# Scan steps moved 1500 places ahead in the scheduler's order, and a back-stage slab that is refilled with the next image pair

## The chip, the cores and the metric

The kernel runs on one core of one Trainium2 chip. The metric is the device time of one execution in microseconds (us). Times of a kernel are given as the median of several runs. A profile is one execution recorded by the hardware profiler; it has a span of its own.

The engines that appear below: PE (TensorE, matrix products; its weight loads are PEld), DVE (VectorE), ACT (ScalarE), POOL (GpSimd), and SP (SyncE), which here only issues DMA transfers.

## What is computed

Four layers are applied to `x` of shape 8 x 64 x 64 x 64 (images, channels, rows, columns), all in float32:

- layer 0: a pixel-attention block with 1x1 and depthwise 3x3 convolutions and batch norms,
- layer 1: two window-attention blocks (8 x 8 windows, 8 heads, the second shifted by 4), each with an MLP,
- layer 2: a dynamic 3x3 filter, then a 1 x 9 convolution,
- layer 3: a selective scan over the 4096 pixels in four directions, a gated norm and projection, then a multi-scale modulation (max pools, depthwise convolutions, GELU).

The scan is the long part. Cut to what matters:

```python
def _selective_scan(xs, dts, A, Bs, Cs, D):
    ...
    def step(h, inp):
        u_t, dt_t, B_t, C_t = inp
        h = h * jnp.exp(dt_t[..., None] * A) + dt_t[..., None] * B_t[:, :, None, :] * u_t[..., None]
        return (h, jnp.einsum('bkcn,bkn->bkc', h, C_t))
    h0 = jnp.zeros(u.shape[1:] + (A.shape[-1],), u.dtype)
    _, ys = jax.lax.scan(step, h0, (u, dt, Bl, Cl))
    return jnp.moveaxis(ys, 0, -1) + D[None, :, :, None] * xs
...
y = out_y[:, 0] + inv[:, 0] + wh + invwh
```

There are 128 channels, 16 states a channel, and 4 directions for each image.

## The kernel before

**Stages.** The eight images are worked in four pairs. A pair passes through `front(p)` (layer0, layer1, layer2, then `scan_sources`, which makes the inputs of the scan: `xc`, its transposed `xt`, and the gate `zs`, all written to DRAM for each image), then `scans(p)` (the selective scan of both images), then `back(p)` (norm, gate, projection and the multi-scale modulation). The main program runs `front(0)` alone and then, for p = 0 to 3, `scans(p)` with other work beside it: `back(p-1)` and then `front(p+1)`, chained in one generator, `beside`. In `scans(3)` there is no front left; `back(2)` lies beside it and `back(3)` is fed in over its last units (`late`) and finished behind it.

**A scan step.** `scans(p)` has 64 units (image, direction k, chunk c of 512 pixels), each of 8 steps, so 512 steps. A step handles two of the 16 states. It consists of two loads by SP that spread one pair of rows over the partitions (B and C, `fetch`, L1801), a product on POOL (`products`, L1809, into `vd`, eight buffers), and in `step`: two exponentials on ACT (L1831), two DVE scan instructions (L1834), two copies of the last column into `carries` on ACT (L1838), and two products with C (L1842), one on POOL and one on DVE; in every fourth step both are on DVE when `own` is 2, which holds for the last two images and while `self.dense` is set. `sums` (L1854) adds the products up on PE in a PSUM bank `yd`. For a unit there are also `load` (the chunk `xs`), `inputs` (two products on PE, exponential and logarithm on ACT, `rows` to DRAM), `spread` (`du`, four transfers) and `gather` (adds `yd` into `Y` on DVE, and in the fourth direction writes `ys`).

**Order.** The code is written in a program order, step by step; the framework's scheduler then places instructions engine by engine. Each instruction has a priority, which is its place in the program. Of the instructions whose inputs and buffers are ready, the scheduler takes the one with the earliest priority. Each engine then executes its queue in the order that was built. `with tc.high_priority(offset=n)` gives the instructions within it a priority n places earlier; it changes no dependence and no amount of work.

In program order `scans` puts, in each step i, the fetches of steps i+3 and i+2, the step, the sums due, and then draws from `beside` as much as its share of the cost: the front and back work spread over all but the last `LEAD` = 24 steps.

**Memory.** `slabs` has three large buffers (128 x 4356 float32). The front and the back stage take them in turn: X, `att`, `VT`, `XP`, `taps`, `H`, `XI`, `XT` in the front; X3, F and `big` in the back stage. A new slab waits until an old one has been released. `layer0` begins with a single 2 MB load of X into a new slab (L1293). `back` loads X3, `y` and `z` by chunks of 512 columns; `y` and `z` lie in the first four eighths of `big`, the same four for each chunk. PSUM banks for the work beside the scans come from the pool `pf` alone; while `front(0)` runs alone (`self.alone`, `turn`), both pools are used and the accumulators of `total` alternate between two banks.

The loop that sets the program order:

Of the kernel before, what the change touches and what calls it, by code (L numbers as in the profile page):

```python
# [18 lines left out]
CH = 512  # L19
# [6 lines left out]
NTD = L // TD  # L26
GRP = 2
LEAD = 24
TC = 1024
NTC = L // TC  # L30
SLAB = 66 * 66
# [1128 lines left out]
class _Direct:  # L1160
# [8 lines left out]
    def __init__(self, net, ctx):  # L1169
        self.net, self.tc, self.nc, self.w = net, net.tc, net.nc, net.w  # L1170
        tc = self.tc
        self.dram = ctx.enter_context(tc.tile_pool(name="mem", bufs=2, space=bass.MemoryType.DRAM))
        self.slabs = ctx.enter_context(tc.tile_pool(name="slabs", bufs=3))
        self.ps = ctx.enter_context(tc.tile_pool(name="ps_scan", bufs=3, space=PSUM))
        self.pf = ctx.enter_context(tc.tile_pool(name="ps_front", bufs=3, space=PSUM))
        self.kept = {}
        self.turn = -1
        self.alone = self.others = False
        self.dense = 0
        self.rows_done = 0  # L1180

    def begin(self, ctx):

# [98 lines left out]
    def front(self, p):  # L1282
# [2 lines left out]
        yield from self.layer2(X)  # L1285
        yield from self.scan_sources(p, X)

    def layer0(self, p):


        nc, tc, w, net, half = self.nc, self.tc, self.w, self.net, self.HALF
        X = self.flat("X")
        nc.sync.dma_start(X, self.net.x[2 * p : 2 * p + 2].rearrange("b c h w -> (b c) (h w)"))  # L1293
        att = self.padded("att")
        VT = self.flat("VT").rearrange("p (t c) -> p t c", c=P)

        def at(rows, t):
            return X[rows, t * P : (t + 1) * P]

        with self.work("w0") as wk:  # L1300
            for g in range(8):
                pv = self.bank("pval", (P, 4, P))
                nc.tensor.matmul(pv, lhsT=net.ones[0:1, :], rhs=net.b1row.rearrange("o a c -> o (a c)").unsqueeze(1).to_broadcast([1, 4, P]), start=True, stop=False)
                for j in range(4):
                    nc.tensor.matmul(pv[:, j, :], lhsT=at(slice(0, P), 4 * g + j), rhs=net.w1bd, start=False, stop=(j == 3))
                nc.scalar.activation(VT[:, 4 * g : 4 * g + 4, :], pv, AF.Relu)
                yield 3

            parts = wk.tile([P, 2, 32, NCH], F32, name="parts", tag="parts", bufs=1)
            self.dense = 1  # L1310
            for jc in range(NCH):
                po = self.total("po")
# [26 lines left out]
                nc.vector.tensor_copy(self.rows(att, jc), self.img(po))  # L1339

            self.dense = 0
            sums = net.sums[:, p]
            nc.vector.tensor_reduce(sums, parts, AX.X, ALU.add)
            rec = wk.tile([P, 2, 32], F32, name="rec", tag="rec", bufs=1)
            nc.vector.reciprocal(rec, sums)
            for g in range(8):
                pr = self.bank("prec")
                for j in range(4):
                    for im in range(2):
                        nc.tensor.matmul(  # L1350
                            pr[half[im], j * P : (j + 1) * P],
                            lhsT=rec[:, im, 4 * g + j : 4 * g + j + 1].to_broadcast([P, 64]),
                            rhs=w["ident"],
                            start=True,
                            stop=True,
                        )
                d = self.rows(att, g)
                nc.vector.tensor_tensor(d, d, self.img(pr), ALU.mult)
                yield 3
        with self.work("w0b") as wk:  # L1360
            diag = self.spread_taps(wk, w["dw2"])
            for c in range(NCH):
                acc = self.bank("cacc", (P, 8, 64))
                yield from self.taps_sum(acc, diag, att, 8 * c, 1.56, wt=w["dw2"], n=5)
                cv = wk.tile([P, 8, 64], F32, name="cv", tag="cv")
                nc.scalar.activation(cv, acc, AF.Relu, scale=net.bn23[:, 0:1], bias=net.bn23[:, 1:2])
                pw = self.bank("pw")
                nc.tensor.matmul(pw, lhsT=w["w3bd"], rhs=cv, start=True, stop=True)
                nc.scalar.activation(pw, pw, AF.Identity, scale=net.bn23[:, 2:3], bias=net.bn23[:, 3:4])
                x = X[:, c * CH : (c + 1) * CH]  # L1370
                nc.vector.tensor_tensor(x, x, pw, ALU.add)
                yield 2.25
        return X
# [339 lines left out]
    def scans(self, p, beside, cost):  # L1713
# [16 lines left out]
        steps = [{} for _ in range(n)]  # L1730
        done = 0
        for i in range(-3, n):
            if i + 3 < n:
                self.fetch(i + 3, steps[i + 3], 0)
            if 0 <= i + 2 < n:
                self.fetch(i + 2, steps[i + 2], 1)
                self.products(i + 2, steps[i + 2])
            if i >= 0:
                self.step(i, steps[i])
                for j in self.DUE[i % 8]:  # L1740
                    if i + j >= 0:
                        self.sums(i + j, steps[i + j], steps[i]["w"])
                if i % 8 == 2 and i > 8:
                    self.gather(self.units[i // 8 - 1])
                if p == B // 2 - 1 and done >= cost:
                    self.turn = max(self.turn, 0)
                while done < cost * (i + 1) / (n - LEAD):
                    done += next(beside, cost)
            if late and i >= n - 8 * (NTD - 1) and i % 8 in (3, 5, 7):
                next(late)  # L1750
            if i >= 0 and i % 8 < 3 and i // 8 + 1 < len(self.units):
                (self.load, self.inputs, self.spread)[i % 8](self.units[i // 8 + 1])
        for i in (n - 2, n - 1):
            self.sums(i, steps[i])
        self.gather(self.units[-1])
# [120 lines left out]
    def back(self, p):  # L1876
        nc, tc, w, net, half = self.nc, self.tc, self.w, self.net, self.HALF
        out = net.out[2 * p : 2 * p + 2].rearrange("b c h w -> (b c) (h w)")
        X = self.flat("X3")
        F = self.padded("F")  # L1880
        big = self.flat("big")
        with tc.tile_pool(name="w4", bufs=2) as wk:
            for c in reversed(range(NCH)):
# [1 line left out]
                nc.sync.dma_start(X[:, cols], self.kept["x", p][:, cols])  # L1885
                po = self.bank("po3")
                for im in range(2):
                    y = self.share(big, im)
                    z = self.share(big, 2 + im)
                    nc.sync.dma_start(y, self.kept["y", 2 * p + im][:, cols])  # L1890
                    nc.sync.dma_start(z, self.kept[2 * p + im][2][:, cols])
                    pc, sd = self.normed(wk, lambda pc: [(pc, y)], w["cen128"], w["avg128"], net.eps[:, 0:1])
                    u = wk.tile([P, CH], F32, name="u", tag="u")
                    nc.vector.scalar_tensor_tensor(pc, pc, w["on_g"], sd, ALU.mult, ALU.mult)
                    nc.vector.scalar_tensor_tensor(u, pc, w["on_b"], z, ALU.add, ALU.mult)
                    nc.tensor.matmul(po[half[im]], lhsT=w["opT"], rhs=u, start=True, stop=True)
                    yield 4.2
# [6 lines left out]
        with tc.tile_pool(name="w5", bufs=1) as wk:  # L1904
# [48 lines left out]
            for c in range(NCH):  # L1953
# [34 lines left out]
                nc.vector.tensor_tensor(pa, pa, self.rows(F, c), ALU.mult)  # L1988
                nc.vector.tensor_tensor(X[:, cols], X[:, cols], pa.rearrange("p a b -> p (a b)"), ALU.add)
                nc.sync.dma_start(out[:, cols], X[:, cols])  # L1990
                yield 3.5
            net.log_exp(last)


# [49 lines left out]
```

## Time and profile before

| | us |
|---|---|
| median of 3 runs | 11730.94 (11729.53 to 11735.17) |
| the profiled execution, reported time | 11724.67 |
| its span in the profile | 11722.8 |
| opening with `front(0)`, until the first scan | 1560 |
| `scans(0)` with `front(1)` | 1560 to 4103 |
| `scans(1)` with `back(0)`, `front(2)` | 4103 to 6872 |
| `scans(2)` with `back(1)`, `front(3)` | 6872 to 9644 |
| `scans(3)` with `back(2)` and `back(3)` | 9644 to 11723 |

Over the span PE is busy 83%, DVE 72%, ACT 60% and POOL 59%. The profile's costliest groups are those of the scan steps; each line shows source line, engine, operation, output from inputs, shapes, count, then busy time and mean duration, then the idle time of the engine just before them and what ended most of it:

```profile
L1809 POOL TENSOR_TENSOR vd<-B,du 128x1024 f32<-128x1024 f32 x2048 | 4801.7, 2363 | 2896.0 <-DMA B<-rows 1732.7
L1842 POOL TENSOR_TENSOR vd<-hd,C 128x512 f32<-128x512 f32 x1737 | 2210.8, 1278 | 1765.4 <-DVE hd L1834 1719.2
L1834 DVE TENSOR_TENSOR_SCAN dad<-dad,carry,vd 128x512 f32<-128x512 f32 x2064 | 2602.0, 1275 | 228.4 <-ACT dad L1831 224.8
L1842 DVE TENSOR_TENSOR vd<-dad,C 128x512 f32<-128x512 f32 x2359 | 1559.6, 673 | 167.9 <-ACT carry L1838 128.7
```

A step thus holds 2.36 us of product on POOL, with 1.28 us more when POOL does one of the two multiplies, and on DVE two scans of 1.27 us and at least one multiply of 0.67 us. A float32 matrix product stands twice in the profile (two passes), so counts of PE rows are twice the program's instructions. "Window rows" below are the 16 calls of `window_row` in a front, eight for each block of layer1.

### The profile page before, as it was taken

The page shows a single profiled execution, that of the slowest core. Times are in us where ns is not written, and L with a number is a line of the kernel's source. Part 1 is how long each engine was busy: PE and PEld are TensorE (multiplying, and loading weights), DVE is VectorE, ACT ScalarE, POOL GpSimd, SP SyncE. Part 2 cuts the span into 40 slices and gives each one's busy share as a digit, 9 for nine tenths or more (in the row PEclk, how much of TensorE's full clock was granted, in tenths as well). Part 3 has the DMA queues.
Part 4 walks back from the last instruction along what each step waited for, and adds up shares of the span by engine and source line. Part 5 has one row for each costly group of instructions (what it writes and reads, how often), then busy time and mean ns, then how long its engine had stood idle before and what let it go on. Part 6 is the DMA issues. An engine that isn't in the chain of part 4 may idle for free. (4 is left out here: it accounts for less than half of the span.)

```text
span 11722.8 us, 161838 instructions
## 1 busy us (share of the span) xinstructions
PE 9682.2 (83%) x55454; PEld 3278.2 (28%) x55454; DVE 8416.8 (72%) x9856; ACT 7078.9 (60%) x16513; POOL 6924.2 (59%) x3799
## 2 busy tenths in 40 slices
PE   9987899998879779998888969999888976655556
PEld 2244332223332222222442213222333221111111
DVE  0033368887777685778777775878778669989998
ACT  5545367766664756776665665776666465555554
POOL 0000058876665565777555574777556558778994
PEclk9998989999999889999999879999998977877677
DMA  0000055553444554555333463555334356556663
GB/s 21 1 2 2 27 164 176 172 174 118 128 124 123 168 165 128 167 169 164 103 113 110 140 201 102 171 166 173 120 106 129 109 172 196 171 177 200 205 205 120
DMA packets 779781, 1577.06 MB, mean 135 GB/s; under 512 B 89280, under 2 KB 89408, under 8 KB 778176
## 3 DMA queue, kind: packets, MB, share of 16 engines
q1 hardware_dynamic: 736320, 1443.18, 40.6%
q10 hardware_dynamic: 42624, 123.44, 3.7%
q8 instruction: 438, 7.18, 0.2%
q14 instruction: 399, 3.27, 0.1%
HBM read 1197.16 MB, written 100.66 MB: 111 GB/s over the span
## 5 line engine op out<-in xcount | busy, mean ns | idle before, releaser
L1809 POOL TENSOR_TENSOR vd<-B,du 128x1024 f32<-128x1024 f32 x2048 | 4801.7, 2363 | 2896.0 <-DMA B<-rows 1732.7
L1842 POOL TENSOR_TENSOR vd<-hd,C 128x512 f32<-128x512 f32 x1737 | 2210.8, 1278 | 1765.4 <-DVE hd L1834 1719.2
L1854 PE MATMUL yd<-vd,pack 128*64 128x512 f32 x8192 | 2684.9, 691 | 602.0 <-POOL vd L1842 501.5
L1831 ACT ACTIVATE dad<-du,As 128x512 f32<-128x512 f32 x4096 | 2719.1, 682 | 635.5 <-DVE vd L1842 412.5
L1834 DVE TENSOR_TENSOR_SCAN dad<-dad,carry,vd 128x512 f32<-128x512 f32 x2064 | 2602.0, 1275 | 228.4 <-ACT dad L1831 224.8
L1834 DVE TENSOR_TENSOR_SCAN hd<-dad,carry,vd 128x512 f32<-128x512 f32 x1520 | 1922.7, 1266 | 347.5 <-ACT dad L1831 298.2
L1842 DVE TENSOR_TENSOR vd<-dad,C 128x512 f32<-128x512 f32 x2359 | 1559.6, 673 | 167.9 <-ACT carry L1838 128.7
L1324 PE MATMUL s<-X 64*128 64x512 f32 x4096 | 1542.2, 644 | 74.9 <-ACT e L1330 68.9
L1330 ACT ACTIVATE e<-s 128x512 f32<-128x512 f32 x2048 | 1197.3, 589 | 468.1 <-PE s L1324 467.8
L1854 PEld LDWEIGHTS yd<-vd,pack 128*64 128x64 f32 x8192 | 651.9, 151 | 2292.6 <-issue 1169.1
L1316 PE MATMUL po<-e,VT 128*64 128x512 f32 x4096 | 1264.5, 620 | 9.5 <-ACT e L1330 8.7
L1838 ACT ACTIVATE carry<-dad 128x1 f32<-128x1 f32 x2063 | 345.8, 169 | 903.4 <-DVE dad L1834 804.4
L1324 PEld LDWEIGHTS s<-X 64*128 64x128 f32 x4096 | 422.2, 186 | 1181.4 <-issue 831.3
L1838 ACT ACTIVATE carry<-hd 128x1 f32<-128x1 f32 x1521 | 303.1, 200 | 678.4 <-DVE hd L1834 669.8
L1483 PE MATMUL w_av<-wide,vals 64*32 64x64 f32 x16384 | 502.6, 227 | 127.3 <-DVE w_oc L1512 74.2
L1483 PEld LDWEIGHTS w_av<-wide,vals 64*32 64x32 f32 x16384 | 416.7, 113 | 258.9 <-issue 138.6
L1316 PEld LDWEIGHTS po<-e,VT 128*64 128x64 f32 x4096 | 250.5, 135 | 841.0 <-issue 565.7
L1471 ACT ACTIVATE wide<-wide 128x512 f32<-128x512 f32 x512 | 310.9, 628 | 287.0 <-DVE wide L1470 287.0
L1494 PE MATMUL w_av<-wide,each 64*32 64x128 f32 x8192 | 474.4, 284 | 8.4 <-issue 8.3
L1243 PE MATMUL pv<-n_sq,pack 128*128 128x512 f32 x576 | 354.7, 700 | 139.6 <-ACT n_sq L1241 127.0
L1771 PE MATMUL pdd<-xs,xdt 128*128 128x512 f32 x512 | 343.7, 758 | 122.3 <-DVE hd L1834 64.2
L1330 ACT ACTIVATION_READ_ACCUMULATOR e<-s 128x1 f32 x2048 | 406.7, 199 | 0.0
(258 smaller groups left out, 10839.1 us busy)
## 6 DMA issues: line engine op xcount, KB each, us to landing
B<-rows SPq DMA_DIRECT2D x2048, 256.0 KB, 3.6
C<-rows SPq DMA_DIRECT2D x2048, 256.0 KB, 3.5
du<-du SPq DMA_DIRECT2D x384, 512.0 KB, 5.5
du<-du ACTq DMA_DIRECT2D x128, 512.0 KB, 5.2
xs<-xt SPq DMA_DIRECT2D x128, 256.0 KB, 3.7
xs<-xc SPq DMA_DIRECT2D x128, 256.0 KB, 3.8
xc<-xcv ACTq DMA_DIRECT2D x64, 256.0 KB, 2.0
xt<-XT ACTq DMA_DIRECT2D x32, 512.0 KB, 5.9
```

The costliest lines, as they stand in the source:

```text
L1243: nc.tensor.matmul(pv, lhsT=avg, rhs=sq, start=True, stop=True)
L1316: nc.tensor.matmul(po[half[im]], lhsT=VT[:, t, half[im]], rhs=es[im], start=(t == 0), stop=(t == 31))
L1324: nc.tensor.matmul(ss[im], lhsT=at(half[im], t), rhs=X[half[im], jc * CH : (jc + 1) * CH], start=True, stop=True)
L1330: nc.scalar.activation(e, ss[im], AF.Exp, scale=C**-0.5, accum_out=parts[:, im, t, jc : jc + 1])
L1483: nc.tensor.matmul(self.av[rows, 0, x % 4 + j], lhsT=net.vals[half[im], x + j, 4 * g + h], rhs=es[g][half[im], j, h], tile_position=(64 * ...
L1494: nc.tensor.matmul(self.av[rows, 1, x % 4 : x % 4 + 2], lhsT=net.each[half[im], 32 - HD - HD * h : 64 - HD - HD * h], rhs=es[g][half[im], ...
L1809: self.nc.gpsimd.tensor_tensor(v, self.twice(st["B"]), self.units[i // 8]["du"][:, :, 1], ALU.mult)
L1831: nc.scalar.activation(da, u["du"][:, j, 0], AF.Exp, scale=net.As[:, k, n : n + 1])
L1834: nc.vector.tensor_tensor_scan(along(to), along(da), along(v[:, j]), first, ALU.mult, ALU.add)
L1838: nc.scalar.activation(self.carries[:, n : n + 1], ends, AF.Copy)
L1842: m = engine.tensor_tensor(v[:, j], hs[j], CC, ALU.mult)
L1854: m = nc.tensor.matmul(u["y"][self.HALF[j]], lhsT=w["fold"], rhs=st["v"][:, j], start=(i % 8 == 0), stop=(i % 8 == 7))
```

## The change

Three things are edited.

1. In `scans`, everything of a step (fetches, products, step, sums, gather) and the preparation of the next unit (`load`, `inputs`, `spread`) is put under `high_priority(offset=AHEAD)` with `AHEAD` = 1500. What is drawn from `beside` keeps its priority, and so does `late`.
2. In `back`, `y` and `z` of even and odd chunks use different halves of `big`.
3. `back(p)` takes the X of `front(p+2)`: as each chunk of X3 has been written to `out`, the chunk before it is loaded from the next image pair, and the slab is handed on through `self.coming`. `layer0` uses it and makes its own load only where there is none.

```diff
+AHEAD = 1500
...
     def layer0(self, p):
...
-        X = self.flat("X")
-        nc.sync.dma_start(X, self.net.x[2 * p : 2 * p + 2].rearrange("b c h w -> (b c) (h w)"))
+        X, self.coming = self.coming, None
+        if X is None:
+            X = self.flat("X")
+            nc.sync.dma_start(X, self.source(p))
...
         for i in range(-3, n):
-            if i + 3 < n:
-                self.fetch(i + 3, steps[i + 3], 0)
-            if 0 <= i + 2 < n:
-                self.fetch(i + 2, steps[i + 2], 1)
-                self.products(i + 2, steps[i + 2])
+            with self.tc.high_priority(offset=AHEAD):
+                if i + 3 < n:
+                    self.fetch(i + 3, steps[i + 3], 0)
+                if 0 <= i + 2 < n:
+                    self.fetch(i + 2, steps[i + 2], 1)
+                    self.products(i + 2, steps[i + 2])
+                if i >= 0:
+                    self.step(i, steps[i])
+                    for j in self.DUE[i % 8]:
+                        if i + j >= 0:
+                            self.sums(i + j, steps[i + j], steps[i]["w"])
+                    if i % 8 == 2 and i > 8:
+                        self.gather(self.units[i // 8 - 1])
             if i >= 0:
-                self.step(i, steps[i])
-                for j in self.DUE[i % 8]:
-                    if i + j >= 0:
-                        self.sums(i + j, steps[i + j], steps[i]["w"])
-                if i % 8 == 2 and i > 8:
-                    self.gather(self.units[i // 8 - 1])
                 if p == B // 2 - 1 and done >= cost:
                     self.turn = max(self.turn, 0)
                 while done < cost * (i + 1) / (n - LEAD):
                     done += next(beside, cost)
...
             if i >= 0 and i % 8 < 3 and i // 8 + 1 < len(self.units):
-                (self.load, self.inputs, self.spread)[i % 8](self.units[i // 8 + 1])
+                with self.tc.high_priority(offset=AHEAD):
+                    (self.load, self.inputs, self.spread)[i % 8](self.units[i // 8 + 1])
...
     def back(self, p):
+        following = self.source(p + 2) if p + 2 < B // 2 else None
...
-                    y = self.share(big, im)
-                    z = self.share(big, 2 + im)
+                    y = self.share(big, 4 * (c % 2) + im)
+                    z = self.share(big, 4 * (c % 2) + 2 + im)
...
                 nc.sync.dma_start(out[:, cols], X[:, cols])
+                if following is not None and c:
+                    old = slice((c - 1) * CH, c * CH)
+                    nc.sync.dma_start(X[:, old], following[:, old])
                 yield 3.5
+            if following is not None:
+                nc.sync.dma_start(X[:, cols], following[:, cols])
+                self.coming = X
```

`source(p)` is the view of `x` that `layer0` loaded before.

More of the change, by code (lines that the diff above doesn't have):

```diff
@@ L1180, in __init__ @@
         self.rows_done = 0
+        self.coming = None
     def begin(self, ctx):
@@ L1286, in front, with source @@
         yield from self.scan_sources(p, X)
+    def source(self, p):
+        return self.net.x[2 * p : 2 * p + 2].rearrange("b c h w -> (b c) (h w)")
     def layer0(self, p):
         nc, tc, w, net, half = self.nc, self.tc, self.w, self.net, self.HALF
-        X = self.flat("X")
-        nc.sync.dma_start(X, self.net.x[2 * p : 2 * p + 2].rearrange("b c h w -> (b c) (h w)"))
+        X, self.coming = self.coming, None
+        if X is None:
+            X = self.flat("X")
+            nc.sync.dma_start(X, self.source(p))
         att = self.padded("att")
```

## The prediction

> **What bounds the kernel now.** I read the busy shares by slice first, then the stretches of each stage, then the number of scans in them. L1834 issues two scans for each step, so half its count is steps. A stage is `scans(p)`, 512 steps; the stages start at 1560, 4103, 6872 and 9644 us (every 1024th scan).
>
> ```profile
> PE   9987899998879779998888969999888976655556
> DVE  0033368887777685778777775878778669989998
> POOL 0000058876665565777555574777556558778994
> PEclk9998989999999889999999879999998977877677
> ```
>
> PE is nearly full while the front runs, and drops to 5 or 6 tenths in the last stage, where DVE takes over. The stretches of stage 0, then of the last stage:
>
> ```profile
> core 0: us, PE busy (x) PEld busy (x) DVE busy (x) ACT busy (x) POOL busy (x), PEclk, DMA share, GB/s
> 1560.00:2737.00 1177.00, 1111.18 (x3592) 323.35 (x3590) 987.37 (x1055) 832.02 (x2320) 951.45 (x517) 0.97 0.59 174
> 2737.00:3505.00 768.00, 630.99 (x8708) 289.49 (x8708) 584.14 (x744) 519.34 (x1062) 459.19 (x257) 0.93 0.41 119
> 3505.00:4103.00 598.00, 493.87 (x1212) 156.86 (x1212) 432.25 (x512) 334.07 (x624) 335.64 (x190) 0.86 0.47 144
> 9644.00:10684.00 1040.00, 647.51 (x1469) 154.96 (x1470) 942.38 (x1008) 564.88 (x1264) 838.86 (x450) 0.76 0.61 185
> 10684.00:11338.00 654.00, 376.67 (x865) 82.68 (x864) 630.84 (x673) 341.41 (x840) 620.38 (x337) 0.70 0.68 206
> ```
>
> The same stretches, L1834 alone (busy, count, clock, DMA):
>
> ```profile
> 1560.00:2737.00 1177.00, 707.61 (x577) 0.97 0.59 174
> 2737.00:3505.00 768.00, 312.10 (x255) 0.93 0.41 119
> 10684.00:11338.00 654.00, 465.20 (x384) 0.70 0.68 206
> ```
>
> Scans beside layer0: 1177/288 = 4.08 us a step, PE 94% busy. Scans beside the window rows of layer1: 768/127.5 = 6.02. Scans with nothing beside them: 654/192 = 3.41, DVE 96% and POOL 95% busy. So layer0 rides along at 0.67 us a step, with all engines well used: this is the overlap that the kernel lives on.
>
> The front with nothing beside it is seen in the opening, before the first scan: layer0; the last two of 16 window rows; eight chunks of `mlp`; layer2; `scan_sources` up to the end of the first image's `xt` issues.
>
> ```profile
> 20.00:640.00 620.00, 614.82 (x2364) 172.86 (x2364) 41.96 (x60) 346.41 (x1064) 0.00 (x0) 1.00 0.01 4
> 1069.00:1128.00 59.00, 45.24 (x1070) 28.49 (x1059) 26.23 (x56) 24.67 (x47) 0.00 (x0) 0.91 0.01 2
> 1128.00:1202.00 74.00, 51.91 (x98) 12.40 (x98) 12.49 (x21) 50.92 (x65) 0.00 (x0) 0.75 0.02 8
> 1202.00:1393.00 191.00, 178.34 (x510) 72.77 (x510) 73.88 (x108) 36.77 (x64) 0.00 (x0) 0.96 0.03 11
> 1393.00:1460.00 67.00, 59.74 (x134) 24.00 (x132) 30.84 (x48) 37.66 (x54) 0.00 (x0) 0.99 0.13 49
> ```
>
> In these 391 us (last four lines) DVE works 143 and POOL nothing.
>
> **What the change does to the order.** The two programs' instruction orders can be compared as built. The raised priority covers every instruction of a step (two loads on SP, POOL's product, ACT's exponentials and carries, DVE's scans and multiplies, PE's sums) and of the next unit's preparation. The amounts of work do not change; their places do:
>
> - Steps 0 to 296 of stage 0 have about 3.1 front instructions between them, where there were 6.2. In stages 1 and 2 the first 272 steps have only the back stage and the rest of `scan_sources`; layer0, which began at step 56 of the stage, begins near step 256.
> - The delayed layer0 comes in a lump: 658 of its 1699 instructions within 16 steps in stage 0, 1144 within 24 steps in stages 1 and 2.
> - Between the last step of a stage and the first of the next, where there were 13 to 18 other instructions, there are now about 1300: two of the 16 window rows, eight `mlp` chunks, all of layer2, and `scan_sources` for the first image. The next scans read that image's `xc`/`xt`, and every older scan is done, so nothing can lie beside this tail. It occurs three times.
>
> **Costs.** All in one execution's time (span 11722.8, reported 11724.67, 6 us below the median 11730.94).
>
> Thin steps, one scan step with little beside it. Bounds 3.41 (above) and 4.08 (layer0's row). For steps that give DVE one multiply in four more (dense ones, as in the 3.41 row) I take 3.65: steps 9644 to 10684, dense with the back stage beside them, still took 1040/256 = 4.06. For the others POOL alone needs 2.36 + 1.28 = 3.64, so I take 3.85, with bounds 3.64 and 4.09 (steps 512 to 544, 131 us).
>
> Lumps of layer0. 620/1699 = 0.365 us an instruction alone; the 103 us before 4516, with 231 of layer0 and 8 steps, give 0.446. I take 0.40, steps included.
>
> Window rows. 768 less 127.5 steps at 3.85 leaves 277 us for 16 rows; 14 rows are 242 on top of the steps. Bounds 150 (thinner mixing) and 300.
>
> Tail. 391 alone. The opening uses two pools of PSUM banks and a second accumulator (`alone`), the tail one; layer2's spreading waits more, 0 to 80 us, I take 24. The restart (load of `xs` 3.7, `rows` 2.2, first B 3.6 to landing, some 15 of matmuls, exponentials and `du` between) is 25. Together 440, bounds 406 and 520.
>
> Stage 0: 296 steps (256 at 3.65, 40 at 3.85) 1088; lump 658 x 0.40 = 263; 32 steps with the convolution at 4.8 (before: steps 264 to 296, 154 us) 154; 164 steps at 3.85 and 14 rows 631 + 242 = 873; tail and its 4 steps 455. Sum 2833, before 2543: +290.
>
> Stage 1: 32 x 3.85 + 240 x 3.65 = 999; 24 steps with 276 of layer0 110; lump 1144 x 0.40 = 458; 32 convolution steps 154, with 40 for layer0's last 100; 156 x 3.85 + 242 = 843; tail 455. Sum 3059, before 2769: +290. Stage 2 likewise, against 2772: +287.
>
> Stage 3: its first 256 steps 256 x 3.65 = 934 in place of 1040: -106. The rest, 1039 us of scans and the last back stage, stays.
>
> The slab edits. One 2 MB load of X (8.0 us to landing, 9.2 from issue to first matmul) goes twice; 16 chunk loads come instead, at 0.33 us of SP each, past which B and C loads queue. Layer0 is no longer awaited at that place, so 0; -18 if it were. Each chunk's load waits on SP for the `out` store of the chunk before it, long landed; the last waits about 2.1 us, covered by B's four buffers (at worst +4 in all). The second pair of shares for `y` and `z` hides a 4.3 us load per half chunk in work already beside the scans; at the very end at most -9. I take 0 for all.
>
> Table loads: 19 more on ACT.
>
> ```profile
> L1831 ACT ACT_TABLE_LOAD x79 | 101.4, 1283 | 17.0 <-DMA xt<-XT 9.0 <-issue 4.9 <-ACT z L1693 2.2
> ```
>
> 19 x 1.283 = 24 us on an engine 60% busy: 0, if exposed 24. The Trainium skill (ScalarE: Activation LUTs, What ACT_TABLE_LOAD costs) counts a drain too, 2.66 us a switch; by that it would be an estimated 51 us, still on ACT.
>
> The clock: granted 0.97 beside layer0 and 0.70 in the scan-only row. The Trainium skill (TensorE: Matmul & The Clock Gate, What's actually happening) lets an idle window halve the clock, which speaks against spreading matmuls thinly; by it the some 900 layer0 instructions of stage 0's thin steps would take twice as long (estimate), though PE has the room.
>
> Sum: +290 +290 +287 -106 = +761, so 12486 for the profiled execution and about 12490 for the median.
>
> **The rivals.**
> - *Milder slowdown (12100).* With fewer bursts beside them the rows cost half: 3 x 121 = -363; 12490 - 363 = 12127. For it: DVE in the 768 us is only 76% busy. Against: the rows still stand in solid blocks of 500 to 1000 instructions at unit boundaries, as before. Dense thin steps at 3.41 (992 x 0.24 = -238) would by themselves give 12250.
> - *Heavier (12750 to 13080).* The back stage's table switches and its DVE work keep dense thin steps at 4.0 (992 x 0.35 = +347), and the tail, with one pool of banks, costs 520 (3 x 80 = +240). For it: 4.06 in stage 3 now. Against: 3.41 with nothing beside.
> - *Faster (11200 to 11600).* The scan is what sets the end and, put first, runs at its floor with the rows filling gaps: dense thin 3.41 (-238), others 3.64 (580 x 0.21 = -122), rows free (-726), lumps at 0.365 (2946 x 0.035 = -103). Sum -1189, so 12490 - 1189 = 11300. Place: the window-row steps. It decides, with those floors met, once the rows cost under about 143 us a stage (761 - 463 = 298, a third of it off 242).
> - *It does not do what it says.* A tail overlapped after all, or nothing moved: the instruction order excludes it nearly; the time would stay at 11730.
>
> **How the numbers follow.** Forecast (12250 to 12750) 0.50, milder (11950 to 12250) 0.21, heavier 0.18, faster 0.08, unchanged 0.03. The measurement can tell about 0.2%, 23 us, from no change. Slower 0.50 + 0.21 + 0.18 = 0.89. Single bounds give: dense thin steps -238/+347 (to 4.0), the other 580 -122/+139, layer0 -103/+136, rows -276/+174, tails -102/+240. Not all fall on one side; taken as independent (root of squares) -411/+497, and the range of 11950 to 12900 takes in the milder case and most of the heavier.
>
> **What would show it.** Right: scans that stop for some 400 us before each of the three later stages, with DVE and POOL nearly idle there; by the sums stage 0 thins until 2650, lumps layer0 until 2910 and has its gap from about 3950 to 4390. PE well under 75% busy in the first 270 steps of stages 1 and 2, at 3.4 to 3.9 us a step, and then some 450 us in which PE is full and 24 steps run. Stage 3 about 100 us shorter. Wrong: no gap between stages, thin steps still over 4 us, or scans beside the rows at under 4.5 us a step. The number most likely off is the rows' 242.

## The result and the profile after

The changed kernel takes 13397.76 us (median of 4 runs, 13388.96 to 13404.81); the kernel before took 11733.06 us beside it (4 runs, 11729.53 to 11755.0). The ratio is 1.1418, 95% interval 1.1403 to 1.1432: 1665 us slower, where the prediction had 761. The span of the profiled execution is 13402.9 us.

The busy shares of the changed kernel in 40 slices of its span (tenths):

```profile
PE   9978888898768656999876865799887685673336
DVE  0133488837773788614775388861678448896777
POOL 0000288835760787524574078751457227776663
PEclk9998899899879777999987977899998797786667
```

DVE and POOL now fall to 0 to 3 tenths several times while PE stays busy, and PE has long stretches at 5 to 7 tenths in between: the overlap has come apart. In the last stage PE is at 3 tenths in three slices; before, it was nowhere under 5 there.

The stages now start at 1566, 4401, 7684 and 10963 us. The stretches of stage 0 (thin steps, the rest of it, the gap behind it), then steps 512 to 768, the lump of layer0 and the gap of stage 1, then the last stage in three parts, each with the busy time and count of every engine:

```profile
core 0: us, PE busy (x) PEld busy (x) DVE busy (x) ACT busy (x) POOL busy (x), PEclk, DMA share, GB/s
1566.00:2641.00 1075.00, 906.08 (x2557) 228.10 (x2556) 945.71 (x1002) 701.00 (x1891) 942.20 (x512) 0.90 0.63 189
2641.00:3924.00 1283.00, 1026.66 (x9120) 372.94 (x9120) 872.62 (x1026) 762.95 (x1791) 787.29 (x442) 0.90 0.41 121
3924.00:4401.00 477.00, 368.00 (x1721) 142.47 (x1722) 154.18 (x243) 168.48 (x250) 12.64 (x10) 0.85 0.09 29
4401.00:5492.00 1091.00, 706.92 (x1599) 180.80 (x1598) 950.02 (x1039) 629.46 (x1334) 855.46 (x460) 0.78 0.61 185
5729.00:6206.00 477.00, 472.84 (x1628) 118.69 (x1624) 83.45 (x87) 281.40 (x858) 86.67 (x49) 0.99 0.13 37
7210.00:7684.00 474.00, 364.71 (x1496) 139.40 (x1497) 151.23 (x238) 165.42 (x245) 16.34 (x12) 0.84 0.09 30
10963.00:12052.00 1089.00, 713.25 (x1587) 182.07 (x1586) 952.27 (x1048) 640.36 (x1345) 841.04 (x452) 0.78 0.60 182
12052.00:12970.00 918.00, 311.29 (x850) 81.46 (x846) 648.62 (x675) 352.44 (x840) 614.28 (x333) 0.65 0.51 151
12970.00:13403.00 433.00, 246.89 (x500) 66.71 (x498) 326.96 (x411) 171.88 (x367) 205.56 (x112) 0.73 0.40 120
```

The scan instructions alone in three of these stretches (DVE busy, count, clock, DMA share, GB/s):

```profile
1566.00:2641.00 1075.00, 706.22 (x577) 0.90 0.63 189
3924.00:4401.00 477.00, 10.11 (x9) 0.85 0.09 29
12052.00:12970.00 918.00, 471.22 (x384) 0.65 0.51 151
```

Three readings. In the 477 us before stage 1 some 4 steps run, POOL works 13 us and DVE 154. In the lump (5729 to 6206) PE is 99% busy and 24 steps run. And the 192 scan-only steps of the last stage, nearly the same work as in the 654 us row of before (DVE 649 us against 631), take 918 us: 4.78 us a step instead of 3.41, with every engine idle for a good part (DVE, the busiest, for 269 us).

The two costliest POOL groups after, and the DVE copy that waits for PE's attention products (busy, mean ns, idle time in front of them and what ended most of it):

```profile
L1819 POOL TENSOR_TENSOR vd<-B,du 128x1024 f32<-128x1024 f32 x2048 | 4797.9, 2360 | 5129.8 <-DMA B<-rows 3012.6
...
L1852 POOL TENSOR_TENSOR vd<-hd,C 128x512 f32<-128x512 f32 x1737 | 2200.4, 1274 | 1210.1 <-DVE hd L1844 1044.8
...
L1346 DVE COPY att<-po 128x512 f32<-128x512 f32 x32 | 21.9, 684 | 1057.3 <-PE po L1323 1057.3
```

POOL's instructions did not become slower (2360 ns against 2363, 1274 against 1278), and its busy time is the same (6920 us, 6924 before). Its loss is idle time: 2234 us more in front of the product and 555 less in front of the multiply, 1679 together. PE's busy time rose by 386 us, to 10068; its granted clock over the whole execution is 0.85, 0.90 before. The copy of `att`, which stood behind 497 us of waiting before, now stands behind 1057: DVE has nothing else to do while PE works through layer0. Table loads rose from 323 to 342, the 19 foreseen.

By stage, from the first scan of one to the first scan of the next (the last to the end of the span):

| us | before | predicted | after | difference to the prediction |
|---|---|---|---|---|
| stage 0 | 2543 | 2833 | 2835 | +2 |
| stage 1 | 2769 | 3059 | 3283 | +224 |
| stage 2 | 2772 | 3059 | 3279 | +220 |
| stage 3 | 2079 | 1973 | 2440 | +467 |

### The profile page after: what moved, and what is told of

Same layout as the page of the kernel before. It is cut to its first block, busy times and chain, and to the rows that moved or that the text cites. A ratio compares the mean times of both kernels' runs of the same rounds, so it can differ in the third digit from the quotient of the medians.

```text
span 13402.9 us, 162552 instructions
## 1 busy us (share of the span) xinstructions
PE 10067.7 (75%) x55454; PEld 3265.5 (24%) x55454; DVE 8441.2 (63%) x9856; ACT 7200.5 (54%) x16532; POOL 6919.5 (52%) x3799
## 5 line engine op out<-in xcount | busy, mean ns | idle before, releaser
L1819 POOL TENSOR_TENSOR vd<-B,du 128x1024 f32<-128x1024 f32 x2048 | 4797.9, 2360 | 5129.8 <-DMA B<-rows 3012.6
L1864 PE MATMUL yd<-vd,pack 128*64 128x512 f32 x8192 | 2945.0, 727 | 1366.4 <-POOL vd L1852 1005.8
L1852 POOL TENSOR_TENSOR vd<-hd,C 128x512 f32<-128x512 f32 x1737 | 2200.4, 1274 | 1210.1 <-DVE hd L1844 1044.8
L1331 PE MATMUL s<-X 64*128 64x512 f32 x4096 | 1418.2, 646 | 37.1 <-ACT e L1337 37.0
L1781 PE MATMUL pdd<-xs,xdt 128*128 128x512 f32 x512 | 417.8, 910 | 648.2 <-ACT carry L1848 380.4
L1331 PEld LDWEIGHTS s<-X 64*128 64x128 f32 x4096 | 385.1, 186 | 1054.2 <-issue 847.7
```

The lines of the kernel that those rows point to most:

```text
L1331: nc.tensor.matmul(ss[im], lhsT=at(half[im], t), rhs=X[half[im], jc * CH : (jc + 1) * CH], start=True, stop=True)
L1781: nc.tensor.matmul(pd, lhsT=net.xdt[:, k, :], rhs=x, start=True, stop=True)
L1819: self.nc.gpsimd.tensor_tensor(v, self.twice(st["B"]), self.units[i // 8]["du"][:, :, 1], ALU.mult)
L1852: m = engine.tensor_tensor(v[:, j], hs[j], CC, ALU.mult)
L1864: m = nc.tensor.matmul(u["y"][self.HALF[j]], lhsT=w["fold"], rhs=st["v"][:, j], start=(i % 8 == 0), stop=(i % 8 == 7))
```

## The experiments

Two questions: what in the change makes the loss, and why stages 1 to 3 lose more than the sums gave. The built orders had shown something that the diff doesn't: `high_priority` sets the scheduler's counter back by `AHEAD`, and on leaving sets it to where it was on entering. Two raised blocks with nothing drawn between them therefore start at the same place, and their instructions tie. That gives two effects to tell apart. *Lead:* some 1500 places counted in front work alone, so that the front lags by that much and its end runs by itself. *Mixing:* instructions of successive steps in an order that is no longer step by step.

In all kernels below, "own places" means that a raised block uses up its places in the counter:

```python
@contextmanager
def raised(self, offset):
    tc, at = self.tc, self.tc.cur_priority
    with tc.high_priority(offset=offset):
        yield
        used = tc.cur_priority - (at - offset)
    tc.cur_priority = at + used
```

**The slab edits alone.** In the changed kernel:

```diff
-            with self.tc.high_priority(offset=AHEAD):
+            if True:
```

in both places.

> The slab edits without the raise. Theory (the raise makes all of the loss): 11690 to 11760, as before, the two whole loads of X gone (9.2 us each from issue to first matmul, partly hidden). Rival (the chunk loads of X that queue on SP ahead of B and C, or the larger share of big, cost): over 11900, stages 1 and 2 longer than 2769 and 2772 us by 100 or more.

Measured 11736.43 us against 11721.97, ratio 1.001 (1.0001 to 1.002). The slab edits bring nothing and cost nothing that matters.

**The raise alone.** Slab edits taken back, raise kept:

```diff
-        X, self.coming = self.coming, None
-        if X is None:
-            X = self.flat("X")
-            nc.sync.dma_start(X, self.source(p))
+        X = self.flat("X")
+        nc.sync.dma_start(X, self.source(p))
```

and in `back` `following = None` and the same four eighths of `big` for every chunk.

> The raise without the slab edits. Theory (the raise makes all of the loss): 13350 to 13450. Rival (slab edits cost): lower than the changed kernel by what they cost, 13200 or less.

Measured 13387.9 us, ratio 1.1417 (1.1394 to 1.144): the whole loss, as expected.

**The raise with own places.** Lead and mixing both change:

```diff
-            with self.tc.high_priority(offset=AHEAD):
+            with self.raised(AHEAD):
```

in both places.

> The changed kernel, but raised blocks take up places of their own in the program's count, so two blocks never stand at the same place; the raise is still 1500 places, now counted over scan and front together. Theory (two causes: blocks that restart at one place mix the steps, and the front's tail of some 1300 instructions runs alone): scan-only steps of the last stage back at 3.4 us, last stage 2070 to 2120; the tail holds some 400 instructions (end of layer2, scan_sources), so gaps of 150 to 220 us in place of 475; total 11900 to 12300. Rival (the last stage is slow for another reason, and being raised is the cause as such): last stage still over 2350, total over 12700.

Measured 12125.44 us, ratio 1.034 (1.0317 to 1.0363). The gaps between stages are 199, 209 and 213 us (477, 474 and 478 in the changed kernel), since raised work now counts among the 1500 places and only some 400 front instructions are left behind the scans. The scan-only steps are at 3.43 us again; the last stage, at 2140, is a little over the 2120 expected. Three quarters of the loss go away, though the same blocks are raised by the same 1500.

**No raise in the last stage.** There is no front beside stage 3, only `back`:

```diff
-            with self.tc.high_priority(offset=AHEAD):
+            with self.tc.high_priority(offset=AHEAD) if p < B // 2 - 1 else nullcontext():
```

> The changed kernel with no raise in the last stage, which has no front beside it. Theory (the mixed order of raised steps makes its 4.78 us a step): scan-only steps back at 3.4, last stage 2040 to 2100 in place of 2440, total 13000 to 13080. Rival (the slow steps come from what stands before, such as late slabs or a back stage that is behind): last stage stays over 2350, total 13350 or more.

Measured 13090.52 us, ratio 1.1163 (1.1141 to 1.1186); stage 3 takes 2137 us instead of 2440 and its scan-only steps 3.41 us. The stage and the total are somewhat over the theory's 2100 and 13080. So 300 us of the loss arise in a stage that has no front, where the raise can only disturb the order among the scans themselves and against `back`. All of it lies behind the stage's first 256 steps. Those took 1098 us without the raise (1089 with it), still more than the 1040 of before:

```profile
10950.00:12048.00 1098.00, 696.04 (x1581) 176.27 (x1579) 965.24 (x1050) 602.29 (x1309) 841.37 (x450) 0.78 0.60 184
```

**Mixing without lead.**

```diff
-AHEAD = 1500
+AHEAD = 0
```

Blocks still start at a shared place wherever nothing is drawn between them.

> The changed kernel with a raise of 0 places: no lead over the front, but raised blocks still restart at the same place. Theory (mixing alone costs, apart from the lead): no gap between stages beyond 40 us, scan-only steps of the last stage at 4.7 to 4.8 us, last stage 2350 to 2450, total 12030 to 12300. Rival (mixing hurts only together with the lead): 11700 to 11800, scan-only steps at 3.4.

Measured 12611.56 us, ratio 1.0756 (1.0735 to 1.0778), worse than both expectations. The scan-only steps are at 4.83 us, and the steps beside layer0 went to 4.70 us, where before has 4.08. I come back to those below.

**Lead without mixing.** `raised` as above with

```diff
-AHEAD = 1500
+AHEAD = 3000
```

so that 1075 to 1163 front instructions are left behind each stage's scans, near the changed kernel's 1308 to 1321.

> As the run with places of its own, but the raise is 3000 places, which leaves 1075 to 1160 front instructions behind each stage's scans (1310 in the changed kernel), so the lead is about that of the changed kernel without its mixing. Theory: gaps of 400 to 460 us, last stage about 2140, stages 1 and 2 near 3000 to 3060 (the prediction's sum), total 12400 to 12700; the rest up to the changed kernel's 13398 is then mixing. Rival (the long lead alone makes the loss): 13000 or more.

Measured 12588.55 us against 11726.43, ratio 1.0737 (1.0715 to 1.0758), as the theory had it. The gap of stage 0 and the scan-only steps in this kernel, columns as in the stretches above:

```profile
3860.00:4307.00 447.00, 352.43 (x1278) 130.09 (x1279) 146.31 (x228) 159.46 (x232) 12.87 (x10) 0.86 0.09 31
...
11517.00:12174.00 657.00, 363.24 (x867) 80.77 (x864) 633.65 (x677) 344.60 (x840) 617.79 (x335) 0.74 0.68 210
```

The gap is there (447 us, POOL 13 us busy) and the scan-only steps run at 3.42. A lead nearly as long as the changed kernel's costs 862 us alone; about 809 more in the changed kernel come from something else.

**Where the scan-only steps lose.** The transfers that SP issues, some of the rows of the timeline: start, duration, queue, line, transfer, how many in a row. First the kernel before:

```profile
10906.50 2.82 SPq L1801 DMA_DIRECT2D B<-rows  x2
10909.44 1.18 SPq L1801 DMA_DIRECT2D C<-rows  x2
...
10922.28 2.35 SPq L1801 DMA_DIRECT2D B<-rows  x3
...
10925.83 1.20 SPq L1801 DMA_DIRECT2D C<-rows  x2
```

The changed kernel:

```profile
12413.17 4.04 SPq L1811 DMA_DIRECT2D B<-rows  x2
...
12420.19 7.44 SPq L1811 DMA_DIRECT2D B<-rows  x4
12429.03 11.27 SPq L1811 DMA_DIRECT2D C<-rows  x8
```

Before, B and C loads alternate in ones to threes. After, the built order has runs of up to eight B loads and then eight C loads, because the blocks of a unit's steps start at one place. A B load waits until POOL's product has read its buffer; while it waits, the C loads behind it on SP wait with it. Who waits for whom, in 800 us of the changed kernel's last stage, SP's own queue first (engine and what it would do, released by; us in total, times, longest):

```profile
SPq L1811 <- POOL vd L1819: 359.4, 148, 6.1
...
ACT dad L1841 <- DVE hd L1844: 249.4, 110, 5.7
...
POOL vd L1819 <- PE yd L1864: 145.8, 29, 6.9
...
DVE hd L1844 <- POOL vd L1819: 127.9, 86, 4.6
POOL vd L1852 <- DMA C<-rows: 99.5, 26, 5.4
```

POOL stands 99.5 us before its second multiply for a C row; the scans behind it, then the exponentials, wait in turn.

**Mixing with the loads in order.** `AHEAD = 0`, the fetches in a block of their own with own places, the rest still sharing:

```diff
-            with self.tc.high_priority(offset=AHEAD):
+            with self.raised(AHEAD):
                 if i + 3 < n:
                     self.fetch(i + 3, steps[i + 3], 0)
                 if 0 <= i + 2 < n:
                     self.fetch(i + 2, steps[i + 2], 1)
+            with self.tc.high_priority(offset=AHEAD):
+                if 0 <= i + 2 < n:
                     self.products(i + 2, steps[i + 2])
```

> The run with a raise of 0 places, but the loads of B and C have places of their own again, so SP issues them alternately; products, scans, multiplies and sums are still in blocks that restart. Theory (mixing costs through SP's queue: eight C loads stand behind eight B loads): scan-only steps at 3.4 to 3.6, last stage under 2200, total within 11700 to 11900. Rival (mixing costs through late multiplies and sums on POOL, DVE and PE): scan-only steps stay over 4.4, last stage over 2330.

Measured 12325.56 us, ratio 1.0512 (1.0491 to 1.0533). The scan-only steps come back from 4.83 to 3.59 us, so SP's order is what they lost by, nearly all of it. The steps beside layer0 stay at 4.71, and so the total missed the theory's 11900, though the last stage (2153 us) met it: those steps have another cause.

**The steps beside layer0: sums in order too.** As the last kernel, and `sums` taken out of the restarting block:

```diff
-                    for j in self.DUE[i % 8]:
-                        if i + j >= 0:
-                            self.sums(i + j, steps[i + j], steps[i]["w"])
+            if i >= 0:
+                for j in self.DUE[i % 8]:
+                    if i + j >= 0:
+                        self.sums(i + j, steps[i + j], steps[i]["w"])
+                with self.tc.high_priority(offset=AHEAD):
                     if i % 8 == 2 and i > 8:
```

> As the run with the loads in their own places, and now the sums stand in program order too, outside the blocks that restart; products, scans and multiplies still mix. In the built order both halves of a sum stand next to each other again in 252 of 252 steps of stage 0's layer0 phase, where that run had 41 of 251. Theory (split pairs of half-width products are what makes the layer0 steps 4.75 us): layer0 steps at 4.0 to 4.15, total 11720 to 11850. Rival (late multiplies and products make them slow): layer0 steps stay over 4.5, total over 12150.

Measured 11778.66 us against 11722.36, ratio 1.0049 (1.0033 to 1.0066), as expected; 4.13 us a step beside layer0. The sums are PE products of 64 columns; two of them use the two halves of PE's array. In the built order of stage 0's first 256 steps, the two halves of a pair are neighbours 252 times of 252 before, 41 of 251 with shared sums, 252 of 252 here. 600 us of those steps, the sums' products (`yd`) and layer0's scores (`s`) on PE: count, busy time in all, mean ns of one, idle time before them. The kernel before:

```profile
L1324 PE MATMUL s<-X 64*128 64x512 f32 x604 | 255.3, 641 | 14.2 <-ACT e L1330 14.2
...
L1854 PE MATMUL yd<-vd,pack 128*64 128x512 f32 x604 | 181.7, 599 | 0.0
```

with the sums shared (only the loads own):

```profile
L1331 PE MATMUL s<-X 64*128 64x512 f32 x510 | 253.4, 644 | 1.2 <-ACT e L1337 1.2
L1874 PE MATMUL yd<-vd,pack 128*64 128x512 f32 x502 | 231.9, 619 | 0.0
```

and with the sums in order:

```profile
L1876 PE MATMUL yd<-vd,pack 128*64 128x512 f32 x580 | 169.4, 600 | 0.0
```

One product lasts as long as ever, some 600 to 620 ns. But 604 of them hold PE for 181.7 us, 0.30 us each, because two run at a time; with pairs apart 502 hold it for 231.9, 0.46 each; with the sums in order it is 0.29 again. Layer0's scores go the same way, 0.42 and 0.50 us each. PE is busy 585 us of the 600 before and 599 with the sums shared, and does less in them (1584 rows for 1886). The starts show the pairs too: of the sums' products in these 600 us, 79% start within 0.12 us of another product before, 59% with the sums shared and 81% with them in order. The Trainium skill (TensorEngine Tiling (Array Packing), Tiling Modes) states that different tiles of the array can execute in parallel, while a change of the tiling mode drains the engine. The 0.30 us of PE time for a product of 600 ns agrees with the first; whether drains add to the loss no run here shows apart.

This explains the two kernels with `AHEAD = 0`, and little of the changed kernel: there the halves of 1679 of 2048 pairs stand together, and the same group holds PE for 224.4 us with 656 products, 0.34 each, in a stretch where PE isn't full.

**Pairs split in the kernel before.** The second half of every pair written behind the drawn work:

```diff
-                        self.sums(i + j, steps[i + j], steps[i]["w"])
+                        self.sums(i + j, steps[i + j], steps[i]["w"], (0,))
...
                     done += next(beside, cost)
+                for j in self.DUE[i % 8]:
+                    if i + j >= 0:
+                        self.sums(i + j, steps[i + j], None, (1,))
```

> The kernel before, no raise and no slab edits, with the second half of each sum written after the work drawn from the front in that step. The built order keeps both halves adjacent in 96 of 252 of stage 0's layer0 steps (before: 252 of 252) and leaves the pairs of layer0 as they were. Theory (a split pair costs PE time where PE is full, about 0.5 us each by the 360 more split pairs and 178 us of the run with a raise of 0 in stage 0): layer0 steps of stage 0 at 4.25 to 4.45, total 11850 to 12080. Rival (adjacency does not matter): 11700 to 11780, layer0 steps at 4.0 to 4.1.

Measured 11774.24 us, ratio 1.0041 (1.0027 to 1.0055): the rival's figure, and the theory missed. The pairs were apart (96 of 252 neighbours) and yet the steps took 4.08 us. But the edit did not take the products' neighbours away: the second half of one step stands next to the first half of the following one, mostly with no drawn work between. In the trace of 1700 to 2300 us, 350 of 595 products start within 0.12 us of another sum's product and 51 within that of one of layer0's products `po`; the group holds PE for 186.9 us with 596, 0.31 each. So this run shows that the pair as such doesn't count. That what counts is a neighbour that can run beside the product fits it, and was not tested by itself. If products of PE that start within 0.12 us of each other are taken as one turn, the traces have 1648 turns in steps 576 to 768 before, 1723 here, 1649 with the sums in order and 1877 with them shared; those steps take 800, 810, 822 and 929 us. The count tells the bad order from the good ones, and no more than that.

**A short lead with own places.** `raised` with

```diff
-AHEAD = 1500
+AHEAD = 100
```

> Places of their own and a raise of 100, some three steps: the listing keeps the front beside the scans to the end of each stage. Theory (the scan first among near equals costs nothing and may gain; the loss is lead and mixing): 11650 to 11800. Rival (any raise of the scan costs PE work beside it): over 11850.

Measured 11966.49 us against 11726.43, ratio 1.0209 (1.0192 to 1.0226). The time rises with the lead, 11966, 12125 and 12589 us at 100, 1500 and 3000 places. The theory's figure was missed and the rival's bound passed: even at 100 the steps beside the front cost more (4.16 us in stage 0's first 288, 4.08 before). Where these 240 us come from stays open.

**Spreading the front sooner.** The own-places kernel with 1500, and

```diff
-LEAD = 24
+LEAD = 72
```

so that the front's program places end 72 steps before the stage does.

> As the run with places of its own and a raise of 1500, but the front is drawn 48 steps earlier (LEAD 72), which leaves 166 to 177 front instructions behind each stage's scans in place of 389 to 418. Theory (work left alone behind the scans is the cost of the lead): gaps of 80 to 130 us in place of 199 to 213, total 11820 to 12000. Rival (the lead costs by delaying PE work, wherever it ends): 12080 or more.

Measured 12095.92 us, ratio 1.032 (1.0298 to 1.0343), the rival's figure. The gaps fell from 199, 209 and 213 to 85, 86 and 91 us, some 360 us in all, and the total by 30: the work that no longer ran in the gap made steps longer elsewhere (the first 288 of stage 0 took 1259 us, 1142 with `LEAD` = 24).

**The changed kernel with its loads in order.** The split of the fetches as above, all else sharing places, `AHEAD = 1750` so that the front lies as in the changed kernel:

```diff
-AHEAD = 1500
+AHEAD = 1750
```

> The changed kernel with one thing mended: the B and C loads of a step take places of their own, all other raised work still shares places from step to step, and the raise is 1750 instead of 1500 so that the front lies where it lies in the changed kernel (1326 front instructions between two stages' scans, 1308 to 1321 there; products of the sums paired 1626 times of 2048, 1679 there). Theory: what the changed kernel loses beyond its lead (about 809 us against the kernel in which all raised work has its own places and the raise is 3000) is the order of B and C loads on SP. Then the scan-only steps of the last stage go from 4.78 back to 3.4 to 3.6 us, that stage from 2440 to 2130 to 2200 (-240 to -310), stages 1 and 2 lose 120 to 200 each, stage 0 up to 90: 12550 to 12850 in all, with the gaps between the stages unchanged at 465 to 485 us. Rival: the mixing of products, multiplies and sums among steps costs by itself; scan-only steps stay above 4.2, and the time above 13050.

Measured 12998.32 us (two runs, 12983 and 13013), ratio 1.1077 (1.1038 to 1.1115): between the two. The last stage did nearly as the theory said:

```profile
10808.00:11901.00 1093.00, 719.03 (x1580) 182.28 (x1578) 953.53 (x1047) 635.59 (x1337) 837.43 (x449) 0.77 0.60 184
11901.00:12586.00 685.00, 392.45 (x862) 90.60 (x862) 632.90 (x672) 352.44 (x840) 622.10 (x337) 0.74 0.66 199
```

The scan-only steps took 685 us for 918 (3.57 a step), and stage 3 2204 for 2440. The stages with a front gained only 40, 61 and 52 us, not 120 to 200. The steps beside the back stage (first line: 1093 us) didn't gain at all. So SP's order costs about 400 us of the 1665, most of it where nothing else lies beside the scans; some 410 us remain between this kernel and the one with the lead alone (12589), of which the gaps (475, 475 and 480 us, 448, 454 and 459 there) make some 70. The rest goes to the sharing of all other places or to the front, which lies deeper here; no run tells those apart. In stages 1 and 2 most of it lies in the first 352 steps (1935 and 1933 us, 1806 and 1802 with the lead alone), above all where layer0 comes in its lump (392 us for 24 steps, 212 there). That speaks for the front's depth, and doesn't show it.

No kernel of these beats the kernel before.

## Why the prediction was right and wrong

**The lead was foreseen, and sized well.** By its own marks: the scans stop before each of the three later stages, for 474 to 478 us with 4 steps (455 foreseen); stage 0 thins until 2674 (2650), has its lump until 2931 (2910) and its gap from 3924 to 4401 (3950 to 4390). Its sum was 2833 and it took 2835. Term by term: the thin steps 1108 (1088), the lump 257 (263), the convolution's steps 149 (154), the 164 steps with the window rows 845 (873). The lumps of stages 1 and 2 were given 458 us and took 477 and 473. The rows' 242, named as the number most likely off, held: 845 less 631 for steps at 3.85 is 214. That stage 0 came out within 2 us is luck in part, as its terms missed by -28 to +22 and cancelled. So is the nearness of 862, the loss with the lead alone, to the sum's 761: that kernel's stage 0 was 88 us under its sum and its stage 3 169 over. And one of the prediction's own signs of being wrong came up: thin steps over 4 us, in stages 1 to 3.

**The step that failed first: "For steps that give DVE one multiply in four more (dense ones, as in the 3.41 row) I take 3.65".** It held beside thin layer0 in stage 0 (3.73 us over the first 288 steps), and not beside the back stage. Steps 512 to 784 took 1157 us and steps 1024 to 1296 1162, 4.25 and 4.27 a step, where the sum had 999 for each. The first 32 of each held (115 us, 123 in the sum); the 240 dense ones took 1042 and 1047, 4.34 and 4.36 a step. Stage 3's first 256 steps took 1089 instead of 934, 4.25 again. The prediction had the right row in hand: steps from 9644 to 10684, dense with the back stage beside them, "still took" 4.06. It let the scan-only row outweigh it, though there was no front beside those 256 steps for a raise to push away. Nor does the raise in that stage set these steps: they took 1098 us without it, 1094 with the loads in order, 1070 and 1071 with own places (leads of 1500 and 3000), 1042 with a lead of 100, and in no run under 1023. The "-106" of stage 3 was thus wrong in sign whatever else the change did. Something of the front does lie in them: the lag leaves the end of `scan_sources` to these steps, among it 32 DVE instructions that did not lie there before:

```profile
L1279 DVE SCALAR_TENSOR_TENSOR xacc<-XI,pack,xacc 128x512 f32<-128x512 f32 x32 | 23.0, 749 | 1.5 <-PE xacc L1277 1.2
```

How much of the 49 us over the 1040 of before that makes is not shown. These thin steps and the 24 after them in stages 1 and 2 (171 and 168 us, 110 foreseen) make 158 + 163 + 155 + 61 + 58 = 595 of the 913 us by which the stages exceed their sums. The rival "heavier" had this very price, 4.0 for dense thin steps; it put it on 992 steps with +347. What holds the thin steps beside the back stage at 4.1 to 4.4 us stays open: in the changed kernel DVE is 87% busy in them and PE 65%.

**The second: "The rest, 1039 us of scans and the last back stage, stays".** The scan-only steps cost +265 (919 for 654) and the end +47 (432 for 385), 312 together. The step took a raised scan to keep its own order. It doesn't: raised blocks share their places, and on SP the loads of later steps went ahead of the C loads of earlier ones. Shown from three sides: 4.83 us a step with shared places and no lead, 3.41 with no raise in that stage, 3.57 with the loads alone put in order. The end's 47 goes without the raise (385) and stays with the loads in order (426), so it has another cause, which stays open. The prediction had compared the built orders, but counted front instructions between the steps, and not the order of the scans' own instructions on each queue.

**The other prices.** The slab edits at 0: shown by the run with them alone (ratio 1.001). The table loads at 0 to 24: nothing shows of them. In the first 256 steps of stage 3 the changed kernel has 66 and the one with no raise there 35, and these steps took 1089 and 1098 us. On the clock: it was granted at 0.90 beside thin layer0 (0.97 before). The Trainium skill's rule on idle windows (TensorE: Matmul & The Clock Gate, What's actually happening) weighed against thin steps; those of stage 0 came out at 3.73 where 3.65 was taken, 23 us over 288 steps, and the clock granted over them, 0.90 in the mean, is far from half.

**The rivals.** "Milder" and "faster" rested on rows that would cost half or nothing; the rows cost 214 of 242, and both fall. "Heavier" came nearest. Its dense thin steps at 4.0 were still too cheap, its tails at 520 too dear (474 to 478), and it had no term for the 312 us of the second step. The stated range ended at 12900, under the 12987 (12490 + 497) that the prediction's own bounds gave; the measured 13398 lies above both.

## What to carry to other kernels

A raise moves work relative to what is not raised, and the delayed work has to run somewhere: where the front's end has no scan left to lie beside, it makes a gap. With the lead alone three gaps came to 1361 us (85 before); the thinner steps gave part of that back, and 862 us were lost. Spreading the front sooner moved 360 us of gap for a gain of 30. When a change raises blocks of a loop, compare the order of the raised instructions among themselves, queue by queue, the DMA-issuing one first: blocks that restart at one place are no longer in step order. And where the trace has a row for the very combination that remains (scans with the back stage, 4.06), it decides over a cleaner row (scans alone, 3.41).

## What had not been expected of the hardware

Half-width products on PE cost half as much again when the order parts them from a neighbour that uses the other half: 0.46 us of PE time instead of 0.30, though each lasts the same 600 to 620 ns in the profile. Beside layer0 a step took 4.71 us in that order, 4.08 before and 4.13 with the sums alone put back in order. It shows neither as a wait nor in a mean duration, only in the busy time of the group divided by its count. A half of another step seems to serve as well as the pair's own second half (4.08 us and 0.31 us a product with 96 of 252 pairs together).
